# Attention input turned by VectorE and DRAM, score row spread by DMAs through DRAM, in a four-layer graph network

## Chip, cores and metric

One core of one Trainium2 chip. The metric is device microseconds of the whole kernel, taken as the median of several runs. Four chips served the experiments; each kernel was compared with the kernel before on the same chip (its medians there: 1815.4 to 1816.4 us).

Engine names: TensorE (PE in the profile, PEld for its weight loads), VectorE (DVE), ScalarE (ACT), GpSimd (POOL), SyncE (SP, the engine that issues nearly all DMAs here).

## The reference, cut

32 batches of 512 tokens with 128 features, everything in fp32, one adjacency matrix of 512 x 512. Each layer is `x = x + layer(relu(layernorm(x)))`.

- layer 0: normalised adjacency times input times a 128 x 128 matrix (GCN)
- layer 1: five steps of a gated recurrence; each step multiplies by the adjacency and applies three gates (GGNN)
- layers 2 and 3: attention over neighbours (GAT)

```python
h = jnp.einsum('bnf,fo->bno', x, W)
e_src, e_dst = h @ a_src, h @ a_dst                       # one score per token each
e = leaky_relu(e_src[:, :, None] + e_dst[:, None, :], 0.2)
e = where(adjacent, e, -inf)
out = softmax(e, -1) @ h
```

## The kernel before

A small scheduler in the kernel, run at build time, gives each operation an assumed cost and delay and lays down a fixed order for every engine. An engine works through its order, so one whose next instruction waits is idle, whatever stands behind it.

```python
plan = Plan({
    "bank": tiles(5, TOKENS, "bank", psum),               # single PSUM banks
    "cand": tiles(1, TOKENS, "cand", psum),
    "wide": tiles(1, [P, C, 2 * P], "wide", psum),        # a double bank, for attention
    "sq": tiles(2, ...), "far": tiles(4, [Q, W, Q, W * C], "far", dram),
    ...
```

The recurrent state (feature-major) gets back to token-major like this in every step: VectorE turns 32 x 32 blocks into `sq`, four DMAs write them to DRAM (`far`), a fifth reads them back in the right place (`h`).

```python
nc.vector.transpose(sq..., new...)
for k in range(Q):
    nc.sync.dma_start(far.t[:, :, k, :].rearrange("q i f -> i q f"), sq.t[k * W:(k + 1) * W])
nc.sync.dma_start(h.t, far.t.rearrange("q i k f -> (q i) k f"))
```

The attention layer turns its input on TensorE and spreads one score per token over all partitions on TensorE too:

```python
pT = to_features(y, ...)                  # 4 transposes on PE, L389, into a bank
gT = nc.vector.tensor_copy(pT)
q = gT @ w_aug                            # "heads": h and three score columns, L495
arg = q[:, :, D:D+3] * rstd;  h[:, :, D:D+3] = exp(arg);  k = h[:, :, D] * rstd
h[:, :, :D] = q[:, :, :D] * k
for c in range(C):                        # 4 transposes on PE, L508, into a bank
    nc.tensor.transpose(row.t[:, c, :], h.t[:, c, D + 2:D + 3].to_broadcast([P, P]), ident.t)
for j in range(C):                        # L511
    e[:, j, :] = max(row, h[:, j, D + 1]) * maskT[:, j, :]
p = e.T @ h                               # "mix", 16 matmuls, L518
```

The softmax here doesn't subtract the row's maximum and nothing guards it: scores larger than these inputs give would overflow.

## Time and profile before

| | before |
|---|---|
| median time, us | 1816.43 |
| span of the profiled run, us | 1814.0 |
| TensorE busy / idle, us | 1773.6 / 40.4 |
| of that idle: first 100 us / middle / after 1700 us | 11.3 / 1.4 / 27.7 |
| VectorE / ScalarE busy | 66% / 37% |
| mean granted TensorE clock | 0.996 |

Idle is the span less the busy time. The lines behind it stand in the prediction and are read there.

### The profile page before, as it was taken

To read this page: it belongs to the slowest core of one execution; us is meant where nothing else is said; L and a number is where in the kernel's file an instruction comes from. 1 tells how busy PE (TensorE), PEld (TensorE's weight loads), DVE (VectorE), ACT (ScalarE), POOL (GpSimd) and SP (SyncE) were. 2 spreads that over 40 slices of the span, in tenths; PEclk is the share of its full clock that TensorE was granted. 3 is DMA by queue.
4 is the path that set the end of the run, shared out by engine and by line. 5 is a ranking of instruction groups with operands and counts; after the bars stand their busy time and mean duration, and the time that the engine had idled before them with its cause. 6 is when DMAs were issued, how large, how long until landed. Compare 5 with 4: busy or idle time off the path is not lost.

```text
span 1814.0 us, 20223 instructions
## 1 busy us (share of the span) xinstructions
PE 1773.6 (98%) x6624; PEld 1143.2 (63%) x6624; DVE 1189.3 (66%) x2981; ACT 672.5 (37%) x1322; POOL 180.4 (10%) x168
## 2 busy tenths in 40 slices
PE   7999999999999999999999999999999999999985
PEld 4555565666665666765766657677666666666665
DVE  8554575577755767854867557677576667665665
ACT  4433344343433344333434334423444233333321
POOL 5100010011100110100111001010001000000000
PEclk9999999999999999999999999999999999999999
DMA  7121212212122212122121222112111221222210
GB/s 227 41 70 53 70 46 59 53 53 53 36 58 67 68 47 53 36 55 61 47 53 41 66 68 54 47 47 60 52 47 53 59 53 47 53 60 57 58 48 18
DMA packets 152266, 103.85 MB, mean 57 GB/s; under 512 B 15328, under 2 KB 131168, under 8 KB 152160
## 3 DMA queue, kind: packets, MB, share of 16 engines
q1 hardware_dynamic: 151872, 102.04, 21.3%
q8 instruction: 52, 0.85, 0.2%
q14 instruction: 54, 0.44, 0.1%
q10 hardware_dynamic: 288, 0.52, 0.1%
HBM read 52.17 MB, written 50.33 MB: 57 GB/s over the span
## 4 chain that ended last, share of the span: by engine, by line
PE 94%; DVE 3%; DMA 1%; issue 0%; POOL 0%; ACT 0%; SPq 0%; DVEq 0%; POOLq 0%; ACTq 0%
PE bank L397 36%; PE wide L518 13%; PE bank L441 8%; PE cand L448 8%; PE cand L449 8%; PE bank L434 8%; PE bank L435 7%; PE wide L495 3%; PE bank L389 2%; PE bank L508 1%; PE bank L413 1%; DVE e L511 1%; DVE st L356 1%; DMA h<-far 0%; DVE off L370 0%
## 5 line engine op out<-in xcount | busy, mean ns | idle before, releaser
L397 PE MATMUL bank<-adjT,h 128*128 128x512 f32 x1280 | 611.5, 605 | 0.6 <-DMA h<-far 0.6
L397 PEld LDWEIGHTS bank<-adjT,h 128*128 128x128 f32 x1280 | 385.7, 311 | 144.7 <-issue 36.0
L453 DVE TENSOR_TENSOR hv<-hv,hT 128x512 f32<-128x512 f32 x160 | 111.1, 694 | 295.3 <-ACT hv L451 294.9
L518 PEld LDWEIGHTS wide<-h_gat,e 128*128 128x128 f32 x2048 | 247.2, 195 | 47.0 <-issue 27.5
L363 POOL TENSOR_TENSOR rstd<-ve,mhalf 128x4 f32<-128x4 f32 x128 | 137.0, 1072 | 1318.4 <-DVE ve L361 367.1
L518 PE MATMUL wide<-h_gat,e 128*128 128x129 f32 x2048 | 250.1, 279 | 11.2 <-DVE h_gat L502 4.1
L399 ACT COPY m<-bank 128x512 f32<-128x512 f32 x192 | 112.1, 584 | 280.9 <-PE bank L397 280.0
L437 ACT ACTIVATE r<-bank,gate_bw 128x512 f32<-128x512 f32 x160 | 109.7, 686 | 260.2 <-PE bank L435 254.8
L439 DVE SCALAR_TENSOR_TENSOR rh<-r,hT 128x512 f32<-128x512 f32 x160 | 109.9, 687 | 137.5 <-ACT r L437 136.6
L511 DVE SCALAR_TENSOR_TENSOR e<-bank,h_gat,maskT 128x512 f32<-128x512 f32 x256 | 175.2, 738 | 13.7 <-PE bank L508 13.4
L443 ACT ACTIVATE z<-bank,gate_bw 128x512 f32<-128x512 f32 x160 | 109.8, 686 | 194.7 <-PE bank L441 194.7
L451 ACT ACTIVATE hv<-cand,gate_bw 128x512 f32<-128x512 f32 x160 | 109.9, 687 | 180.6 <-PE cand L449 180.3
L463 DVE STREAM_TRANSPOSE sq<-hT 128x512 f32<-128x512 f32 x160 | 164.7, 1029 | 4.4 <-DMA far<-sq 1.8
L441 PE MATMUL bank<-m,wT 128*128 128x512 f32 x320 | 163.9, 594 | 1.7 <-ACT r L437 1.7
L434 PE MATMUL bank<-m,wT 128*128 128x512 f32 x320 | 163.8, 593 | 1.4 <-ACT m L399 1.4
L448 PE MATMUL cand<-m,wT 128*128 128x512 f32 x320 | 163.5, 592 | 0.0
L449 PE MATMUL cand<-rh,wT 128*128 128x512 f32 x320 | 163.5, 592 | 0.0
L435 PE MATMUL bank<-hT,wT 128*128 128x512 f32 x320 | 163.4, 592 | 0.0
L397 PE MATMUL bank<-anT,y 128*128 128x512 f32 x256 | 122.8, 607 | 1.6 <-DVE x L415 0.9
L356 DVE BATCH_NORM_STATS2 st<-x 128x6 f32<-128x128 f32 x512 | 117.7, 279 | 1.6 <-DMA x<-in_x_dram 0.8
L456 DVE SCALAR_TENSOR_TENSOR hT<-hv,hT 128x512 f32<-128x512 f32 x160 | 110.3, 689 | 4.0 <-PE bank L441 0.5
L454 DVE SCALAR_TENSOR_TENSOR hv<-z,hv 128x512 f32<-128x512 f32 x160 | 110.2, 689 | 3.9 <-issue 0.2
(85 smaller groups left out, 1418.7 us busy)
## 6 DMA issues: line engine op xcount, KB each, us to landing
far<-sq SPq DMA_DIRECT2D x640, 64.0 KB, 1.8
h<-far SPq DMA_DIRECT2D x160, 256.0 KB, 2.6
x<-in_x_dram SPq DMA_DIRECT2D x32, 256.0 KB, 4.5
out_dram<-x SPq DMA_DIRECT2D x32, 256.0 KB, 2.2
e<-in_adj_dram ACTq DMA_DIRECT2D x2, 256.0 KB, 4.2
e<-in_adj_dram SPq DMA_DIRECT2D x2, 256.0 KB, 3.9
w<-in_L_gnn_w_w_dram SPq DMA_DIRECT2D x3, 128.0 KB, 3.8
u<-in_L_gnn_u_w_dram SPq DMA_DIRECT2D x2, 64.0 KB, 3.0
```

The lines of the kernel that those rows point to most:

```text
L356: op("DVE", 0.21, due, lambda c=c: nc.vector.bn_stats(st.t[:, c, :], xb.t[:, c, :]), r=[xb[c]], w=[st[c]])
L363: op("POOL", 1.0, due, lambda: nc.gpsimd.tensor_tensor(rstd.t, ve.t, mhalf.t, ALU.pow), r=[ve, mhalf], w=[rstd])
L397: op("PE", MM, due, lambda c=c: nc.tensor.matmul(flat(p.t), chunk(h, c), mT.t[:, c, :], start=(c == 0), stop=(c == C - 1)), r=[h[c] if len ...
L399: op("ACT", A, due, lambda: nc.scalar.copy(flat(m.t), flat(p.t)), r=[p], w=[m])
L434: nc.tensor.matmul(flat(gate.t), gates.t[:, 0, :], flat(m.t), start=True, stop=False)
L435: nc.tensor.matmul(flat(gate.t), gates.t[:, 1, :], flat(hT.t), start=False, stop=True)
L441: op("PE", MM, due + 0.3, lambda: nc.tensor.matmul(flat(gate.t), gates.t[:, 2, :], flat(m.t), start=False, stop=True, skip_group_check=Tru ...
L448: nc.tensor.matmul(flat(cand.t), gates.t[:, 3, :], flat(m.t), start=True, stop=False)
L449: nc.tensor.matmul(flat(cand.t), u5T.t[:, 0, :], flat(rh.t), start=False, stop=True)
L463: op("DVE", 0.61 if last else 1.0, due - 5, lambda: nc.vector.transpose(sq.t.rearrange(form, c=C), flat(new.t).rearrange("p (c q i) -> p q ...
L511: op("DVE", 0.68, due + 2, lambda j=j: nc.vector.scalar_tensor_tensor(e.t[:, j, :], flat(row.t), h.t[:, j, D + 1:D + 2], maskT[l].t[:, j, ...
L518: nc.tensor.matmul(p.t[:, c, :D + 1], e.t[:, j, c * P:(c + 1) * P], h.t[:, j, :D + 1], start=(j == 0), stop=(j == C - 1))
```

## The change

The intent is to take 448 transposes off TensorE, which is the bound. In 28 of 32 batches the input of attention takes the way that the recurrent state already takes (VectorE blocks, DRAM, back), and the score row is written to DRAM and read back by all partitions. The last four batches (`near`), whose latency ends the run, keep TensorE. The blocks leave tokens in a permuted order, so masks are permuted once through DRAM; the layer-norm scale moves into the ReLU, which removes two small VectorE operations. With the banks no longer needed for the transposes, two single banks become a second double bank. Only 16 buffers for x remain, to make room in SBUF.

```diff
-        "bank": tiles(5, TOKENS, "bank", psum),
+        "bank": tiles(3, TOKENS, "bank", psum),
-        "wide": tiles(1, [P, C, 2 * P], "wide", psum),
+        "wide": tiles(2, [P, C, 2 * P], "wide", psum),
+        "x": tiles(16, TOKENS, "x"),
+        "row": tiles(2, [P, N], "row"),
+        "line": tiles(4, [C, Q, W], "line", dram),
 ...
+    def shuttle(src, squares, dst, form, due, soon):     # the five DMAs above, as a function
 ...
     def gat(b, l, due):
-        pT = to_features(y, due + 1, gT)
+        near = b >= B - NEAR                              # NEAR = 4
+        if near: pT = to_features(y, due + 1, gT) ...
+        else:    shuttle(y, "p (c q j) -> p q c j", gT, "p q (c j) -> p q c j", due + 0.5, due)
 ...
+        else:
+            line = Val("line", C)
+            for c in range(C):
+                op("SP", 0.4, due + 1.5, lambda c=c: nc.sync.dma_start(
+                    line.t[c].rearrange("q i -> i q"), h.t[c * W:(c + 1) * W, :, D + 2]),
+                   r=[h[1]], w=[line[c]], delay=5)
+            op("SP", 0.4, due + 1.5, lambda: nc.sync.dma_start(
+                row.t, line.t.rearrange("c q i -> (c q i)").unsqueeze(0).to_broadcast([P, N])),
+               r=[line], w=[row, e], delay=4.5)
```

The line, one score column of `h`, four bytes in each of 32 partitions and four slots, goes to DRAM as 128 pieces of 4 bytes. Four such DMAs make one row.

More of the change, by code (lines that the diff above doesn't have):

```diff
@@ L20 @@
 Q = P // W
+NEAR = 4
 LANES = 4
@@ L181, in gnn_stack @@
         "hv": tiles(2, TOKENS, "hv"),
-        "gT": tiles(2, TOKENS, "gT"),
+        "gT": tiles(2, [P, Q, W * C], "gT"),
         "h_gat": tiles(3, [P, C, D + 3], "h_gat"),
+        "row": tiles(2, [P, N], "row"),
+        "line": tiles(4, [C, Q, W], "line", dram),
         "e": tiles(2, [P, C, N], "e"),
         "v": tiles(2, TOKENS, "v"),
+        "mask": tiles(2, [P, N], "mask", dtype=BF16),
         "st": tiles(4, [P, C, 6], "st"),
@@ L190, in gnn_stack @@
         "off": tiles(4, SMALL, "off"),
-        "arg": tiles(3, [P, C, 3], "arg"),
-        "k": tiles(3, SMALL, "k"),
         "rden": tiles(3, SMALL, "rden"),
@@ L230, in gnn_stack @@
     for b in range(B):
-        v = Val(None, C)
-        v.t = tiles(1, TOKENS, f"x{b}")[0]
-        op("SP", 0.95, -995 + b, lambda v=v, b=b: nc.sync.dma_start(v.t, x[b].rearrange("(c p) d -> p c d", p=P)),
+        v = Val("x", C)
+        op("SP", 0.95, max(-995 + b, STEPS * b - 20) if b >= 8 else -995 + b, lambda v=v, b=b: nc.sync.dma_start(v.t, x[b].rearrange("(c p) d -> p c d", p=P)),
            w=[v], delay=3)
@@ L292, in gnn_stack, with edges @@
     op("DVE", 4 * 0.7 + 4 * 0.25, -797, scale_rows, r=[adjT, dinv, drow, ident, dinv2], w=[anT])
-    maskT = {l: fixed([P, C, N], f"maskT{l}", dtype=BF16) for l in (2, 3)}
+    maskT = {l: fixed([P, Q, N], f"maskT{l}", C, dtype=BF16) for l in (2, 3)}
     for l in (2, 3):
-        op("DVE", 1.25, 5 + l, lambda l=l: nc.vector.tensor_scalar(maskT[l].t, adjT.t, 0.0, None, op0=ALU.is_gt),
-           r=[adjT], w=[maskT[l]])
-    def own_edges():
-        for m in range(C):
-            nc.vector.scalar_tensor_tensor(block(maskT[2].t, m), block(adjT.t, m), -1.0, ident.t,
-                                           op0=ALU.mult, op1=ALU.is_lt)
-    op("DVE", 4 * 0.25, 8, own_edges, r=[adjT, ident], w=[maskT[2]])
+        far = Val(None, C)
+        far.t = tiles(1, [Q, W, C, N], f"far_mask{l}", dram, BF16)[0]
+        for c in range(C):
+            part = Val("mask", 1)
+            def edges(l=l, c=c, part=part):
+                nc.vector.tensor_scalar(part.t, adjT.t[:, c, :], 0.0, None, op0=ALU.is_gt)
+                if l == 2:
+                    nc.vector.scalar_tensor_tensor(part.t[:, c * P:(c + 1) * P], block(adjT.t, c), -1.0, ident.t,
+                                                   op0=ALU.mult, op1=ALU.is_lt)
+            op("DVE", 0.35 if l == 3 else 0.6, 4 + l, edges, r=[adjT, ident], w=[part])
+            op("SP", 0.4, 4 + l, lambda c=c, far=far, part=part: nc.sync.dma_start(
+                far.t[:, :, c, :].rearrange("q i n -> (q i) n"), part.t), r=[part], w=[far[c]], delay=2.2)
+        for c in range(C):
+            op("SP", 0.4, 4 + l, lambda l=l, c=c, far=far: nc.sync.dma_start(
+                maskT[l].t[c * W:(c + 1) * W], far.t[:, :, c, :].rearrange("q i n -> i q n")),
+               r=[far], w=[maskT[l][c]], delay=2.2)
     ws = {k: fixed([P, D], k + "s") for k in ("w4", "w3", "w5")}
@@ L391, in to_features @@
         return p
+    def shuttle(src, squares, dst, form, due, soon):
+        sq, far = Val("sq"), Val("far", Q)
+        op("DVE", 0.61 if form == "p q (c j) -> p q c j" else 1.0, soon, lambda: nc.vector.transpose(
+            sq.t.rearrange(form, c=C), flat(src.t).rearrange(squares, c=C, q=Q)), r=[src], w=[sq])
+        for k in range(Q):
+            op("SP", 0.44, due, lambda k=k: nc.sync.dma_start(
+                far.t[:, :, k, :].rearrange("q i f -> i q f"), sq.t[k * W:(k + 1) * W]), r=[sq], w=[far[k]], delay=1.7)
+        op("SP", 0.4, due, lambda: nc.sync.dma_start(dst.t, far.t.rearrange("q i k f -> (q i) k f")),
+           r=[far], w=[dst], delay=2.5)
     def product(h, mT, due):
@@ L460, in step @@
         last = s == STEPS - 1
-        sq, far, h = Val("sq"), Val("far", Q), Val("h")
+        h = Val("h")
         form = "p q (c j) -> p q c j" if last else "p q (j c) -> p q c j"
-        op("DVE", 0.61 if last else 1.0, due - 5, lambda: nc.vector.transpose(
-            sq.t.rearrange(form, c=C), flat(new.t).rearrange("p (c q i) -> p q c i", c=C, q=Q)), r=[new], w=[sq])
-        for k in range(Q):
-            op("SP", 0.44, due, lambda k=k: nc.sync.dma_start(
-                far.t[:, :, k, :].rearrange("q i f -> i q f"), sq.t[k * W:(k + 1) * W]), r=[sq], w=[far[k]], delay=1.7)
-        op("SP", 0.4, due, lambda: nc.sync.dma_start(h.t, far.t.rearrange("q i k f -> (q i) k f")),
-           r=[far], w=[h], delay=2.5)
+        shuttle(new, "p (c q i) -> p q c i", h, form, due, due - 5)
         if last:
@@ L481, in gat @@
     def gat(b, l, due):
-        xb, y, off = xs[b], Val("y", C), Val("off")
-        mv, rstd = norm_stats(b, due)
-        op("DVE", 0.1, due, lambda: nc.vector.tensor_scalar_mul(off.t, mv.t[:, :, 0], -1.0), r=[mv], w=[off])
-        for c in range(C):
-            op("ACT", 0.32, due, lambda c=c: nc.scalar.activation(y.t[:, c, :], xb.t[:, c, :], AF.Relu, bias=off.t[:, c:c + 1]),
-               r=[xb[c], off], w=[y[c]])
-        gT, h = Val("gT"), Val("h_gat", 2)
-        pT = to_features(y, due + 1, gT)
-        op("DVE", V, due + 1, lambda: nc.vector.tensor_copy(flat(gT.t), flat(pT.t)), r=[pT], w=[gT])
-        q, arg, k = Val("wide"), Val("arg"), Val("k")
+        xb, y, gT, h, q = xs[b], Val("y", C), Val("gT"), Val("h_gat", 2), Val("wide")
+        norm_relu(b, y, due)
+        near = b >= B - NEAR
+        if near:
+            pT = to_features(y, due + 1, gT)
+            op("DVE", V, due + 1, lambda: nc.vector.tensor_copy(
+                gT.t.rearrange("p q (c i) -> p q c i", c=C), pT.t.rearrange("p c (q i) -> p q c i", q=Q)), r=[pT], w=[gT])
+        else:
+            shuttle(y, "p (c q j) -> p q c j", gT, "p q (c j) -> p q c j", due + 0.5, due)
         def heads():
@@ L495, in heads @@
                 nc.tensor.matmul(q.t[:, c, :D + 3], gT.t[:, c, :], w_aug[l].t, start=True, stop=True)
-        op("PE", C * MM1, due + 1, heads, r=[gT, w_aug[l]], w=[q, h])
-        op("DVE", 0.1, due + 1, lambda: nc.vector.tensor_mul(arg.t, q.t[:, :, D:D + 3], rstd.t[:, :, None].to_broadcast([P, C, 3])),
-           r=[q, rstd], w=[arg])
-        op("ACT", 0.22, due + 1, lambda: nc.scalar.activation(h.t[:, :, D:D + 3], arg.t, AF.Exp), r=[arg], w=[h[1]])
-        op("DVE", 0.1, due + 1, lambda: nc.vector.tensor_mul(k.t, h.t[:, :, D], rstd.t), r=[h[1], rstd], w=[k])
@@ L502, in gat @@
-        op("DVE", V, due + 1, lambda: nc.vector.tensor_mul(h.t[:, :, :D], q.t[:, :, :D], k.t[:, :, None].to_broadcast([P, C, D])),
-           r=[q, k], w=[h[0]])
-        row, e = Val("bank"), Val("e", C)
-        def spread():
+        op("PE", C * MM1, due + 1.5, heads, r=[gT, w_aug[l]], w=[q, h])
+        op("ACT", 0.22, due + 1, lambda: nc.scalar.activation(h.t[:, :, D:D + 3], q.t[:, :, D:D + 3], AF.Exp), r=[q], w=[h[1]])
+        op("DVE", V, due + 1.5, lambda: nc.vector.tensor_mul(
+            h.t[:, :, :D], q.t[:, :, :D], h.t[:, :, D:D + 1].to_broadcast([P, C, D])), r=[q, h[1]], w=[h[0]])
@@ new lines, in gat, with spread @@
+        row, e = Val("row"), Val("e", C)
+        if near:
+            pr = Val("bank")
+            def spread():
+                for k in range(Q):
+                    nc.tensor.transpose(pr.t[:, k, :], h.t[:, k, D + 2:D + 3].to_broadcast([P, P]), ident.t)
+            op("PE", C * TURN, due + 2, spread, r=[h[1], ident], w=[pr, row])
+            op("ACT", A, due + 2, lambda: nc.scalar.copy(
+                row.t.rearrange("p (c q i) -> p c q i", c=C, q=Q), pr.t.rearrange("p q (c i) -> p c q i", c=C)),
+               r=[pr], w=[row, e])
+        else:
+            line = Val("line", C)
@@ L507, in spread @@
             for c in range(C):
-                nc.tensor.transpose(row.t[:, c, :], h.t[:, c, D + 2:D + 3].to_broadcast([P, P]), ident.t)
-        op("PE", C * TURN, due + 2, spread, r=[h[1], ident], w=[row, e])
+                op("SP", 0.4, due + 1.5, lambda c=c: nc.sync.dma_start(
+                    line.t[c].rearrange("q i -> i q"), h.t[c * W:(c + 1) * W, :, D + 2]), r=[h[1]], w=[line[c]], delay=5)
+            op("SP", 0.4, due + 1.5, lambda: nc.sync.dma_start(
+                row.t, line.t.rearrange("c q i -> (c q i)").unsqueeze(0).to_broadcast([P, N])), r=[line], w=[row, e], delay=4.5)
@@ L510, in gat @@
         for j in range(C):
-            op("DVE", 0.68, due + 2, lambda j=j: nc.vector.scalar_tensor_tensor(
-                e.t[:, j, :], flat(row.t), h.t[:, j, D + 1:D + 2], maskT[l].t[:, j, :], op0=ALU.max, op1=ALU.mult),
+            op("DVE", 0.68, due + 3, lambda j=j: nc.vector.scalar_tensor_tensor(
+                e.t[:, j, :], row.t, h.t[:, j, D + 1:D + 2], maskT[l].t[:, j, :], op0=ALU.max, op1=ALU.mult),
                r=[row, h[1], maskT[l]], w=[e[j]])
@@ L519, in mix @@
                                      start=(j == 0), stop=(j == C - 1))
-            op("PE", C * MM1, due + 3, mix, r=[e, h], w=[p] if c == 0 else [p[c]])
-        op("DVE", 0.12, due + 3, lambda: nc.vector.reciprocal(rden.t, p.t[:, :, D]), r=[p], w=[rden])
+            op("PE", C * MM1, due + 4, mix, r=[e, h], w=[p] if c == 0 else [p[c]])
+        op("DVE", 0.12, due + 4, lambda: nc.vector.reciprocal(rden.t, p.t[:, :, D]), r=[p], w=[rden])
         if l == 2:
             v, n = Val("v"), Val("r")
-            op("DVE", V, due + 3, lambda: nc.vector.tensor_mul(v.t, p.t[:, :, :D], rden.t[:, :, None].to_broadcast([P, C, D])),
+            op("DVE", V, due + 4, lambda: nc.vector.tensor_mul(v.t, p.t[:, :, :D], rden.t[:, :, None].to_broadcast([P, C, D])),
                r=[p, rden], w=[v])
-            op("ACT", A, due + 3, lambda: nc.scalar.activation(flat(n.t), flat(v.t), AF.Exp), r=[v], w=[n])
-            op("DVE", V, due + 3, lambda: nc.vector.scalar_tensor_tensor(flat(v.t), flat(v.t), 0.0, flat(xb.t), op0=ALU.max, op1=ALU.add),
+            op("ACT", A, due + 4, lambda: nc.scalar.activation(flat(n.t), flat(v.t), AF.Exp), r=[v], w=[n])
+            op("DVE", V, due + 4, lambda: nc.vector.scalar_tensor_tensor(flat(v.t), flat(v.t), 0.0, flat(xb.t), op0=ALU.max, op1=ALU.add),
                r=[xb], w=[v])
-            op("DVE", V, due + 3, lambda: nc.vector.scalar_tensor_tensor(flat(xb.t), flat(n.t), 1.0, flat(v.t), op0=ALU.min, op1=ALU.add),
+            op("DVE", V, due + 4, lambda: nc.vector.scalar_tensor_tensor(flat(xb.t), flat(n.t), 1.0, flat(v.t), op0=ALU.min, op1=ALU.add),
                r=[n, v], w=[xb])
@@ L536, in finish @@
                                                    op0=ALU.mult, op1=ALU.add)
-            op("DVE", 4 * 0.28, due + 3, finish, r=[p, rden], w=[xb])
-            op("SP", 0.95, due + 3, lambda: nc.sync.dma_start(out[b].rearrange("(c p) d -> p c d", p=P), xb.t), r=[xb])
+            op("DVE", 4 * 0.28, due + 4, finish, r=[p, rden], w=[xb])
+            op("SP", 0.95, due + 4, lambda: nc.sync.dma_start(out[b].rearrange("(c p) d -> p c d", p=P), xb.t), r=[xb])
     for b in range(B):
@@ L544, in gnn_stack @@
         gat(b, 2, STEPS * b + LANES * (STEPS - 1) + 3)
-        gat(b, 3, STEPS * b + LANES * (STEPS - 1) + 7)
+        gat(b, 3, STEPS * b + LANES * (STEPS - 1) + 8)
     with tc.manual_schedule():
```

## The prediction

> **What bounds the kernel now.** I read, in this order: the busy totals and slices of the page, the table of stretches, the waits of TensorE, its timeline in the middle of the run, the groups by line, and the landing times of the DMAs.
>
> ```profile
> PE 1773.6 (98%) x6624; PEld 1143.2 (63%) x6624; DVE 1189.3 (66%) x2981; ACT 672.5 (37%) x1322; POOL 180.4 (10%) x168
> ...
> 0.00:100.00 100.00, 88.66 (x252) 1.00 0.44 127
> 100.00:1700.00 1600.00, 1598.64 (x5929) 1.00 0.21 54
> 1700.00:1814.00 114.00, 86.25 (x448) 0.93 0.14 38
> ...
> PE bank L434 <- ACT m L399: 0.7, 1, 0.7
> PE bank L397 <- DMA h<-far: 0.6, 2, 0.3
> ```
>
> The reader is to see that TensorE is busy for 1598.64 of the 1600 us from 100 to 1700 us, and that its only waits there are the two last lines, 1.3 us in all. Its idle time is 11.3 us in the first 100 us and 27.7 us in the last 114. So the middle is bound by what TensorE issues and by nothing else, and a TensorE instruction removed there is worth its issue interval, whatever the other engines do, as long as they keep up.
>
> The interval is not the duration in the table. The timeline of TensorE (start, busy, engine, line) shows it:
>
> ```profile
> 1101.01 2.00 PE L397 MATMUL bank<-adjT,h 128*128 128x512 f32 x4
> 1102.84 0.60 PE L508 MATMUL bank<-ident,h_gat 128*128 128x128 f32 x4
> 1103.28 0.60 PE L389 MATMUL bank<-ident,y 128*128 128x128 f32 x4
> 1103.72 1.14 PE L397 MATMUL bank<-adjT,h 128*128 128x512 f32 x2
> 1104.70 1.06 PE L495 MATMUL wide<-w_aug,gT 128*128 128x131 f32 x8
> ```
>
> Four transposes have a mean duration of about 0.27 us each, but the next group starts 0.44 us after the first of the four (1102.84, 1103.28, 1103.72): 0.11 us each. The median over all such groups of four between 60 and 1730 us is 0.44 us for L508 (the score row) and for L389 on y. The last lines show a second cost: two matmuls of L397 on h take 0.98 us to the next group there, and 0.86 us when their predecessor is a 512-column matmul (median of 42 groups). The groups tell why: this line's weights are read with a stride.
>
> ```profile
> L397 PEld LDWEIGHTS bank<-adjT,h 128*128 128x128 f32 x1280 | 385.7, 311 | 144.7 <-issue 36.0
> L453 DVE TENSOR_TENSOR hv<-hv,hT 128x512 f32<-128x512 f32 x160 | 111.1, 694 | 295.3 <-ACT hv L451 294.9
> L518 PEld LDWEIGHTS wide<-h_gat,e 128*128 128x128 f32 x2048 | 247.2, 195 | 47.0 <-issue 27.5
> ```
>
> A load of 311 ns does not fit under a 128-column predecessor, a load of 195 ns shows no such penalty. L453 is here for its idle time: VectorE waits 295 us in front of this one line, so it has room.
>
> **What the skill says.** The Trainium skill, "TensorE: Matmul & The Clock Gate", Part 4: PE-mode transpose, gives about 275 ns for a transpose in a kernel's context. The trace has 273 ns as the median duration, but the interval of 0.11 us decides here. The same page, LDWEIGHTS (loading the stationary operand), makes the load depend on the number of columns alone; the trace differs, 311 against 195 ns for the same 128 columns, and the measurement decides. "VectorE: DVE Perf Modes", The three transpose paths, says that VectorE turns only 32x32 blocks and writes SBUF; that is why the change needs DMAs to put the blocks in place. The trace has 693 ns (contiguous output) and 1099 ns (strided) for a 128x512 turn. "DMA: Bandwidth & Descriptors", Anatomy of one DMA, puts a fixed part of about 2 us before any size effect. The trace agrees: 2.1 us for 0.5 KB, 1.8 us for 64 KB, 2.6 us for 256 KB.
>
> ```profile
> far<-sq SPq DMA_DIRECT2D x640, 64.0 KB, 1.8
> h<-far SPq DMA_DIRECT2D x160, 256.0 KB, 2.6
> ...
> a_pair<-in_L_gnn_a_src_dram SPq DMA_DIRECT2D x2, 0.5 KB, 2.2
> ```
>
> **The change part by part.** There are 64 attention layers, two for each of 32 batches. The last four batches keep the old way, so 56 change.
>
> Removed from TensorE: 56 x (4 + 4) transposes. The built programs confirm it (transposes of y and h_gat go from 256 each to 32 each; nothing is added). 56 x 0.88 us = 49.3 us, all in the stretch that is 99.9% busy.
>
> Removed indirectly: the order of the built programs shows how often L397 on h starts behind a short instruction, 125 times before and 64 times after. 61 x 0.12 us = 7.3 us.
>
> VectorE: each of the 56 loses a gT copy (0.684 us) and gains a square turn (0.69), which is nothing. All 64 lose arg and k (0.162 + 0.171), 21 us. The 256 score operations (L511) read the row from SBUF in place of PSUM; L439, the same kind from SBUF, takes 0.687 us against 0.738, so some 11 us less in the 224 that change. The sum is about -30 us, off the path.
>
> ScalarE: the ReLU takes a scale as well, 391 to some 483 ns for 256 pieces, +24 us on an engine that is 37% busy. Off the path.
>
> DMA: 56 x (4 far + 1 gT + 4 line + 1 row) = 560 more issues of 0.43 us: SyncE's queue goes from 884 to 1460 issues in the built program, some 640 us of issuing in 1760. Traffic grows by 56 x 0.75 MB = 42 MB over 104; at the present cost, a DMA share of 21% becomes about 30%. Hidden, if nothing waits for it.
>
> Does something wait? From the attention's matmul on w_aug ("heads") to its first mix matmul, the new chain is: heads 0.9, exponential 0.2, gaps 0.3, four line issues 1.7, landing 2.1, row 2.6, four score operations 2.8 = 10.6 us (an estimate from the durations above). Counting TensorE work between those two points in the built order, with the intervals measured here, gives 15 to 30 us, median 18, for the 56 changed layers. That is 4 us of margin at the worst. Before, the same count gives 6 to 22 us for a chain of about 5 us, and TensorE did not wait at all in the middle. The order was laid for slower DMAs than these.
>
> PSUM: five single banks become three, but none is used any more for y, and the score row no longer occupies one for four score operations. A GGNN step holds a bank for its product (3.4 us plus the copy) and one for its gates (about 6 us), some 10 bank-us in 7.7 us of TensorE work, so three should do. The second double bank lets the heads of one layer start while another mixes.
>
> The end: before, 6.25 mixes are left behind the last GGNN matmul and 66 us pass, because one double bank passes from layer to layer and VectorE is 98% busy from 1770 to 1780. After, 7 mixes are left, in pairs over two double banks. I give it 3 us less idle time. For waits that I do not foresee in the middle I add 3 us.
>
> Sum: 1816.75 - 49.3 - 7.3 - 3 + 3 = 1760 us, 3.1% less.
>
> **The rivals.** (1) The row's way through DRAM is slower than I count: 512 pieces of 4 bytes per layer, and 128 partitions reading the same 2 KB. If line and row took 5 us each, the chain would be 16 us and the tightest layers would wait a few us each; SyncE and VectorE work in order, so the GGNN steps behind would be held too. 56 layers x 0.5 us gives 1788, "same". Against it: the 0.5 KB loads landed in 2.2 us, and the DMA engines are 21% busy. For it: no DMA of the trace before has this shape. (2) The three banks become the bound: the product of one lane waits for the evacuation of another. The sign would be waits of L421 or L458 for ScalarE. With 0.2 us in each of 160 steps it would be 1792. Against it: before, ScalarE waits for TensorE and not the other way round. (3) Only the removed transposes count and the 7.3 us do not appear, or the pairs in the tail crowd VectorE: 1767 to 1772. (4) The reverse: two double banks shorten the tail by 10 us or more, 1750.
>
> **Range and chances.** The saving of 49.3 us is certain in its count, so the time is 1767 without any second effect. Favourable ones (7 and up to 10 us) pull to 1750, waits push to 1776 before a rival is really at work. The 2% line is at 1780.4, which needs 20 us of new idle time in the middle or at the end; I give that one chance in ten. Slower by 2% would need 92 us of new waits: 0.01.
>
> **What would show it.** Right: TensorE idle under 6 us from 100 to 1700 us, transposes of y and h_gat 32 each, busy time down by some 50 us. Step two: the groups of L421 on h that follow a 512-column matmul are more, and busy time falls by more than 49. Wrong: waits of the mix (L546) for the score operations, themselves waiting for the row DMA; landing times of line and row above 4 us; waits of L421 or L458 for a bank; h landing later than 3.2 us; or more than 30 us idle in the tail.

## The result and the profile after

The changed kernel is correct and slower: 1961.55 us (1955.39 to 1962.28, four runs) against 1816.43, ratio 1.079 with a 95% interval of 1.077 to 1.081. Ratios are the mean time of one kernel's fast runs over that of the other's of the same rounds, so not quite the ratio of the medians. The prediction was 1760 us, with a range of 1750 to 1776.

From the page of the changed kernel and its table of stretches (length, TensorE busy with its count, granted clock, DMA share, GB/s):

```profile
PE 1788.2 (91%) x6176; PEld 1125.6 (57%) x6176; DVE 1180.4 (60%) x2859; ACT 692.7 (35%) x1330; POOL 185.3 (9%) x168
...
100.00:1850.00 1750.00, 1608.53 (x5453) 0.96 0.34 77
1850.00:1960.00 110.00, 91.85 (x473) 0.90 0.16 43
```

The 448 transposes are gone (6624 to 6176 matmuls), yet busy time rose, the middle that was full now has 141 us of idle time, and the granted clock is 0.96 there. The waits of TensorE (waited for, total us, times, longest):

```profile
PE wide L513 <- DMA gT<-far: 45.6, 15, 8.5
PE wide L546 <- DVE e L539: 36.0, 35, 6.0
PE cand L473 <- DVE rh L463: 30.8, 8, 10.8
PE bank L421 <- DMA h<-far: 15.9, 7, 4.6
```

L513 is the heads, L546 the mix, L473 a gate of the recurrence, L421 its product. The waits are spread over four places, of which only L546 belongs to the score row. What they share is seen in the landing times of the DMAs:

```profile
far<-sq SPq DMA_DIRECT2D x864, 64.0 KB, 1.8
h<-far SPq DMA_DIRECT2D x160, 256.0 KB, 2.6
gT<-far SPq DMA_DIRECT2D x56, 256.0 KB, 2.9
row<-line SPq DMA_DIRECT2D x56, 256.0 KB, 3.9
...
line<-h_gat SPq DMA_DIRECT2D x224, 0.5 KB, 7.2
```

The smallest transfer of all is the slowest, 7.2 us for 0.5 KB. And medians hide company. The three lines below are the last line of the view of one source line, for `far` in the kernel before, for `far` after, and for the line DMAs after (minimum, median, maximum):

```profile
DMA to landing us min/median/max: 1.6/1.8/4.2
DMA to landing us min/median/max: 1.6/1.8/11.8
DMA to landing us min/median/max: 5.7/7.2/12.4
```

The worst `far` went from 4.2 to 11.8 us. I sorted the trace's `far`, `h` and `gT` issues after 235 us, grouped as the timeline groups them, by how long after a line DMA they were issued. The numbers are the median over the groups of each group's median landing time:

| issued after the latest line DMA | far, us | h, us | gT, us |
|---|---|---|---|
| within 3 us | 6.3 (28 groups) | 8.1 (7) | 8.4 (8) |
| more than 10 us | 1.8 (140) | 2.6 (71) | 2.8 (25) |

So a DMA that has nothing to do with the score row lands about 5 us late if it stands right behind a line. One place in the timeline shows how this reaches TensorE, and what it costs twice:

```profile
581.25 1.02 PE L472 MATMUL cand<-m,wT 128*128 128x512 f32 x2
593.04 2.08 PE L473 MATMUL cand<-rh,wT 128*128 128x512 f32 x2 [10.77 <-DVE rh L463]
594.91 2.77 PE L421 MATMUL bank<-adjT,h 128*128 128x512 f32 x3
```

The chain of waits in that stretch runs: line DMAs, then `far` DMAs issued behind them that take 6.62 us, then the VectorE turn (L409) that needs the buffer they empty, then `rh`, which stands behind it in VectorE's order, then L473. After the 10.77 us of waiting, two matmuls take 2.08 us in place of 1.02. The Trainium skill, "TensorE: Matmul & The Clock Gate", Part 1: The HAM clock gate, says that the clock falls to half after an idle window of some 3.4 us; the trace agrees, with 2.08 against 1.02 us here and a mean clock of 0.958 over the run. All six matmuls with 512 columns that follow a gap of over 3.4 us in this trace take 1.21 to 1.22 us, twice the 0.61 us that those of L421 take on average. (The length of the window itself was not tested.)

### The profile page after: what moved, and what is told of

Read it like the earlier page. It is cut to its first block, busy times and chain, and to the rows that moved or that the text cites. A ratio compares the mean times of both kernels' runs of the same rounds, so it can differ in the third digit from the quotient of the medians.

```text
span 1959.2 us, 20126 instructions
## 1 busy us (share of the span) xinstructions
PE 1788.2 (91%) x6176; PEld 1125.6 (57%) x6176; DVE 1180.4 (60%) x2859; ACT 692.7 (35%) x1330; POOL 185.3 (9%) x168
## 4 chain that ended last, share of the span: by engine, by line
PE 61%; DMA 22%; DVE 8%; SPq 3%; ACT 3%; issue 2%; POOL 0%; DVEq 0%; ACTq 0%; POOLq 0%
PE bank L421 23%; PE wide L546 9%; DMA line<-h_gat 6%; DMA row<-line 5%; PE cand L473 5%; DMA far<-sq 5%; PE bank L458 5%; PE bank L459 5%; PE bank L465 5%; PE cand L472 5%; DVE e L539 2%; DMA gT<-far 2%; DMA h<-far 2%; DVE sq L409 2%; SPq L534 1%
## 5 line engine op out<-in xcount | busy, mean ns | idle before, releaser
L421 PE MATMUL bank<-adjT,h 128*128 128x512 f32 x1280 | 619.1, 612 | 18.8 <-DMA h<-far 15.9
L421 PEld LDWEIGHTS bank<-adjT,h 128*128 128x128 f32 x1280 | 390.3, 311 | 197.4 <-issue 70.7
L546 PE MATMUL wide<-h_gat,e 128*128 128x129 f32 x2048 | 271.0, 291 | 45.9 <-DVE e L539 36.0
L546 PEld LDWEIGHTS wide<-h_gat,e 128*128 128x128 f32 x2048 | 260.1, 204 | 82.8 <-DVE e L539 46.6
L539 DVE SCALAR_TENSOR_TENSOR e<-row,h_gat,maskT 128x512 f32<-128x512 f32 x256 | 181.8, 755 | 83.3 <-DMA row<-line 82.4
L409 DVE STREAM_TRANSPOSE sq<-hT 128x512 f32<-128x512 f32 x160 | 163.6, 1023 | 69.9 <-DMA far<-sq 66.2
L473 PE MATMUL cand<-rh,wT 128*128 128x512 f32 x320 | 169.3, 611 | 30.8 <-DVE rh L463 30.8
L385 ACT ACTIVATE y<-x,off,rstd 128x128 f32<-128x128 f32 x384 | 161.0, 484 | 60.7 <-DVE sq L409 27.6
L458 PE MATMUL bank<-m,wT 128*128 128x512 f32 x320 | 168.3, 608 | 0.2 <-ACT m L423 0.2
L465 PE MATMUL bank<-m,wT 128*128 128x512 f32 x320 | 165.8, 600 | 0.8 <-ACT r L461 0.8
L513 PE MATMUL wide<-w_aug,gT 128*128 128x131 f32 x512 | 76.4, 298 | 55.3 <-DMA gT<-far 45.6
L473 PEld LDWEIGHTS cand<-rh,wT 128*128 128x128 f32 x320 | 61.5, 195 | 110.7 <-issue 62.9
```

What stands on the lines that cost most here:

```text
L385: op("ACT", 0.32, due, lambda c=c: nc.scalar.activation(chunk(y, c), xb.t[:, c, :], AF.Relu, bias=off.t[:, c:c + 1], scale=rstd.t[:, c:c + ...
L409: op("DVE", 0.61 if form == "p q (c j) -> p q c j" else 1.0, soon, lambda: nc.vector.transpose(sq.t.rearrange(form, c=C), flat(src.t).rear ...
L421: op("PE", MM, due, lambda c=c: nc.tensor.matmul(flat(p.t), chunk(h, c), mT.t[:, c, :], start=(c == 0), stop=(c == C - 1)), r=[h[c] if len ...
L458: nc.tensor.matmul(flat(gate.t), gates.t[:, 0, :], flat(m.t), start=True, stop=False)
L465: op("PE", MM, due + 0.3, lambda: nc.tensor.matmul(flat(gate.t), gates.t[:, 2, :], flat(m.t), start=False, stop=True, skip_group_check=Tru ...
L473: nc.tensor.matmul(flat(cand.t), u5T.t[:, 0, :], flat(rh.t), start=False, stop=True)
```

## The experiments

Thirteen kernels ran. All computed the right result; the probe kernels' total times mean nothing.

### 1. Which part of the change

**a1_row_by_pe**: row spread by TensorE in all batches, input still turned through DRAM.

```diff
-        near = b >= B - NEAR
-        if near:                       # input
+        if b >= B - 4:                 # input
 ...
-        if near:                       # row
+        if True:                       # row
```

> Changed kernel, but the score row is spread by TensorE in all 32 batches; the attention input still goes through VectorE squares and DRAM. T1 (the 4-byte line DMAs are slow and clog the SyncE queue): the loss goes, 24.6 us of the transposes stay saved, so 1785 to 1800 us. T2 (three single PSUM banks are too few): still above 1900. T3 (the way of the attention input through DRAM is what comes late; its waits are the largest, 45.6 us): above 1880.

**a2_turn_by_pe**: the other way round (input `True`, row `b >= B - 4`).

> The other half: the attention input is turned by TensorE in all batches, the score row still goes by line and row DMAs through DRAM. T1: still slow, 1890 to 1960 us, line landing near 7 us. T2: above 1900. T3: back to 1790 to 1800.

**a3_all_by_pe**: both `True`.

> Both by TensorE in all batches, so what is left of the change is three single banks and two double ones, heads in permuted token order, masks through DRAM, 16 x buffers. T1 and T3: 1808 to 1822 us, as before. T2: 1850 or more, with waits of TensorE for ScalarE's evacuations.

**a4_line_512B**: the changed kernel, with one more VectorE operation that puts the 128 scores of each line into one partition. The scheduler's assumed delays stay.

```diff
+            op("DVE", 0.25, due + 1.5, lambda: nc.vector.transpose(
+                cols.t, h.t[:, :, D + 3 - W:]), r=[h], w=[cols])       # 32x32 turns
             for c in range(C):
                 op("SP", 0.4, due + 1.5, lambda c=c: nc.sync.dma_start(
-                    line.t[c].rearrange("q i -> i q"), h.t[c * W:(c + 1) * W, :, D + 2]),
+                    line.t[c].unsqueeze(0), cols.t[(c + 1) * W - 1:(c + 1) * W]),
                    ...
```

> The changed kernel with one addition: a VectorE 32x32 turn (128x128, estimate 0.3 us) puts each score line into one partition, so each of the four line DMAs moves one piece of 512 bytes in place of 128 of 4 bytes; the planned delays stay. T1: line landing 1.8 to 2.5 us, no stalled SyncE issues, 1760 to 1775 us, faster than before by 2 to 3%. T2 or T3: stays above 1880.

| kernel | median, us | ratio to before (95%) | TensorE busy / idle, us |
|---|---|---|---|
| before | 1816.35 | | 1773.6 / 40.4 |
| a1_row_by_pe | 1798.87 | 0.991 (0.989 to 0.992) | 1750.1 / 47.1 |
| a2_turn_by_pe | 1939.23 | 1.067 (1.065 to 1.070) | 1797.1 / 134.4 |
| a3_all_by_pe | 1798.82 | 0.990 (0.989 to 0.992) | 1766.5 / 29.9 |
| a4_line_512B | 1754.35 | 0.966 (0.965 to 0.968) | 1718.7 / 35.3 |

Every kernel with the 4-byte lines is slow, every kernel without them is faster than before (a1 and a3 by 1% only, but clear of the noise). Two expectations missed: a3 came 9 us below its range of 1808 to 1822, and a4 came 6 us below its 1760 to 1775. a4 differs from the changed kernel by the form of the line alone and is 207 us faster. The three single banks (T2) and the input's way through DRAM (T3) are out as causes: both are in a4. Its busy times and the stretch from 100 to 1650 us:

```profile
PE 1718.7 (98%) x6176; PEld 1096.7 (63%) x6176; DVE 1192.8 (68%) x2915; ACT 697.5 (40%) x1330; POOL 183.2 (10%) x168
...
100.00:1650.00 1550.00, 1543.39 (x5458) 1.00 0.32 87
```

TensorE runs the same 6176 matmuls as in the changed kernel in 69.5 us less of busy time (1788.2 - 1718.7): that is the price of the low clock. Busy time times mean clock is nearly the same in both, 1788.2 x 0.958 = 1713 and 1718.7 x 0.996 = 1712. Idle time differs by 135.7 us (171.0 - 35.3). The two make up the 205 us between the spans.

a1 fell in its range, but it gains nothing on a3, though it has 224 transposes fewer: busy time falls by 16.4 us and idle time rises by 17.2. Its order is another one, and I did not find which of its waits is to blame.

### 2. Why a line hurts: late rows, held-up queue, or something below

Three theories. L: only the row comes later than the order expects. S: SyncE issues in order, and the built program hands eight completion semaphores in turn to its DMAs, so slow lines hold up the issue of the next DMAs. J: the lines slow the other DMAs while these are in flight.

**b1_plan_slow**: the scheduler is told that a line lands after 9 us.

```diff
-                   r=[h[1]], w=[line[c]], delay=5)
+                   r=[h[1]], w=[line[c]], delay=9)
```

> The changed kernel, laid out by its scheduler with 9 us in place of 5 for the landing of a line DMA; the program is the same but for order. L (only the late row hurts: the order expects it too early): 1790 us or less. S (a slow line DMA holds up the DMAs behind it in SyncE's order) and J (the small pieces slow the other DMAs themselves): 1850 to 1950.

**b2_dead_lines**: a1 plus the line DMAs, which nothing reads.

> a1_row_by_pe (1799 us) plus the 4-byte line DMAs of 28 batches, which nothing reads. L: 1795 to 1805, since no row waits. S and J: 1860 to 1940, with TensorE waiting for h and gT DMAs and for VectorE.

**b4_one_line_dma**: one DMA for the row's 512 pieces; ScalarE restores the order afterwards.

```diff
-            for c in range(C):
-                nc.sync.dma_start(line.t[c].rearrange("q i -> i q"), h.t[c * W:(c + 1) * W, :, D + 2])
+            nc.sync.dma_start(line.t.rearrange("q p -> p q"), h.t[:, :, D + 2])      # line is [Q, P]
```

> The changed kernel with one line DMA of 512 pieces of 4 bytes in place of four of 128 (and a ScalarE copy of the row that puts it in order). S: a long DMA holds one of the eight completion semaphores and not four, so much returns: 1770 to 1830. J: the same pieces, so 1900 or more. L: 1900 or more if it lands no sooner than 7 us.

**b3_lines_by_pool**: `nc.gpsimd.dma_start` in place of `nc.sync.dma_start` for the lines.

> The changed kernel with the 4-byte line DMAs issued by GpSimd, whose queue and completion semaphores are its own. If the lines only hold up what stands behind them in SyncE's own queue (ring): far and h DMAs land in 1.8 and 2.6 us again, and the time is 1760 to 1800 us. If they hold up the 16 DMA engines as such: far DMAs still land 3 us or more late beside a line, and the time stays above 1880.

| kernel | median, us | ratio to before (95%) | line landing, us |
|---|---|---|---|
| b1_plan_slow | 1948.76 | 1.073 (1.071 to 1.075) | 7.3 |
| b2_dead_lines | 1922.27 | 1.058 (1.057 to 1.060) | 7.0 |
| b4_one_line_dma | 1997.96 | 1.100 (1.096 to 1.103) | 9.9 |
| b3_lines_by_pool | 1912.63 | 1.053 (1.050 to 1.056) | 7.2 |

L falls as the main cause. Telling the order that lines are slow gives back 13 us, and lines that nobody waits for still cost 123 us on top of a1. That leaves 84 of the 207 us, of which late rows may have a part: in the changed kernel TensorE waits 36.0 us for scores (L546). The waits of TensorE in b2 are of the same kind as in the changed kernel, without any row to wait for (here L514 is the heads and L422 the product):

```profile
PE wide L514 <- DMA gT<-far: 41.1, 8, 10.3
PE bank L422 <- DMA h<-far: 27.5, 7, 5.6
```

S falls as the main cause: my expectation of 1770 to 1830 us for a single DMA was wrong by 168 us or more, and lines on GpSimd's queue, with semaphores that SyncE does not use, leave b3 158 us slower than a4. In b3 the `far` groups issued by SyncE within 3 us of a line still land after 7.4 us (median of 24 groups), against 1.8 us more than 10 us away from one. S may have a part in it all the same. b3 gives back 49 us, though its order is another one too, and the waits of SyncE in the changed kernel have this line for `far` issues that need nothing from a line,

```profile
SPq L412 <- DMA line<-h_gat: 53.3, 23, 4.5
```

but what it waits for is the landing itself. So most of the slowdown lies below the issuing queues, in what they share; how much S and L add to it was not parted further.

### 3. What makes the line slow

**m1_probes** and **m2_probes** put probe DMAs ahead of the changed kernel, five of a form, each waiting for the one before of its form (`scatters` and `rows`: four or more in flight). The first of a form does not wait for the last of the form before it, so it may run beside it.

```diff
+    probe("column", [P, 1], ..., lambda t, k: nc.sync.dma_start(t, msrc.t[:, 0, D + 2:D + 3]))
+    probe("apart",    [P, 16], ...,  dma_start(t[:, :1], msrc.t[:, 0, D + 2:D + 3]))     # 64 B apart
+    probe("farapart", [P, 128], ..., dma_start(t[:, :1], msrc.t[:, 0, D + 2:D + 3]))     # 512 B apart
+    ...
```

> The changed kernel with DMA probes in front of everything (the time means nothing): each form five times, one after the other. Forms: one line DMA as the kernel has it (128 pieces of 4 bytes, SBUF to DRAM), four of them in flight as in the kernel, 128 pieces of 4 bytes to a contiguous column, 128 pieces of 16 bytes, four rows of 512 bytes, the row spread to 128 partitions, and a load of 128 pieces of 4 bytes. If the number of pieces written makes the line slow: scatter and column and quads alike, 4 us or more alone, rows about 2 us. If it is only the company of other DMAs: all about 2 us alone, and slow only with four in flight. Spread 2.6 to 4 us; the load 2.1 us, as in the trace of before.

> Probes again, one DMA at a time, each form five times, read by the distance between issues. The first probes gave 8.0 us for 128 pieces of 4 bytes in a column of DRAM, 3.3 us for 128 pieces of 16 bytes, 2.2 us for the same 4-byte column loaded. Now: 4-byte pieces side by side, 64 bytes apart and 512 bytes apart, 32 pieces only, pieces of 8, 16, 32, 64 and 512 bytes, and 4-byte pieces into SBUF. If each small write is slow by itself: 8 us also when apart, 3 to 4 us for 32 pieces. If small writes hinder their neighbours in one block of DRAM: about 2.5 us when 512 bytes apart. In both cases about 2 us into SBUF and for 512 bytes.

From SyncE's timeline in m1 (start, first to last issue, form): the kernel's own line form alone, and four of them in flight at a time.

```profile
1.44 28.26 SPq L243 DMA_DIRECT2D scatter<-msrc  x5
29.74 29.93 SPq L244 DMA_DIRECT2D scatters<-msrc  x20
```

One alone takes (28.26 - 0.3)/4 = 7.0 us from issue to issue, on an idle chip, and four in flight take no longer (five rounds in 29.93 us). It is slow by itself, not by company. m1 also had 128 pieces of 16 bytes, which I took for 3.3 us each; the first of them ran beside the last 4-byte column and waited 8.3 us, the others took 1.4 to 1.8. So the number of pieces does not make the line slow. The row alone took 3.0 to 3.3 us, the 4-byte load 1.9 to 2.0 (first ones left out). From the DMA view of m2 (pieces written, KB, median us from issue to landing):

```profile
lines<-msrc SPq DMA_DIRECT2D x5, 64.0 KB, 1.5
...
column<-msrc SPq DMA_DIRECT2D x5, 0.5 KB, 8.8
apart<-msrc SPq DMA_DIRECT2D x5, 0.5 KB, 1.4
farapart<-msrc SPq DMA_DIRECT2D x5, 0.5 KB, 1.4
quarter<-msrc SPq DMA_DIRECT2D x5, 0.1 KB, 5.4
pairs<-msrc SPq DMA_DIRECT2D x5, 1.0 KB, 3.4
quads<-msrc SPq DMA_DIRECT2D x5, 2.0 KB, 2.0
beats<-msrc SPq DMA_DIRECT2D x5, 4.0 KB, 1.4
blocks<-msrc SPq DMA_DIRECT2D x5, 8.0 KB, 1.4
onchip<-msrc SPq DMA_DIRECT2D x5, 0.5 KB, 1.7
```

| 128 pieces unless noted, to DRAM | form | us |
|---|---|---|
| 4 B, side by side | column | 8.8 |
| 4 B, 64 B apart | apart | 1.4 |
| 4 B, 512 B apart | farapart | 1.4 |
| 4 B, side by side, only 32 pieces | quarter | 5.4 |
| 8 B, side by side | pairs | 3.4 |
| 16 B, side by side | quads | 2.0 |
| 32 B and 64 B, side by side | beats, blocks | 1.4 |
| 512 B, side by side | lines | 1.5 |
| 4 B into SBUF | onchip | 1.7 |

Medians are needed here, because the first DMA of a form runs beside the last of the form before. The first `apart` was issued 0.36 us after the last `column` on the same queue, and landed only after it, as its minimum, median and maximum show:

```profile
DMA to landing us min/median/max: 1.4/1.4/8.9
```

That is the delay of section 2 on an otherwise idle chip: a DMA that takes 1.4 us lands after 8.9 behind a column of single words.

The same number of 4-byte pieces takes 8.8 or 1.4 us, and what decides is how near to each other they fall in DRAM. The first branch of what I expected (each small write is slow by itself) is out; the second holds (1.4 us at 512 B, where I had expected 2.5), and already 64 B apart, or with pieces of 32 B, the cost is gone. The Trainium skill, "DMA: Bandwidth & Descriptors", Specifications, says that below 512 B the DMA engine does a read-modify-write. No run here shows that step itself; 4-byte writes 64 or 512 B apart and 32-byte writes side by side land as soon as 512-byte ones, so a write below 512 B is not slow as such, only close beside others. That they wait for one another's turn at a block of DRAM would fit the numbers; it is argued, not shown.

**b5_dead_lines_apart**: b2 with the unread pieces 512 B apart; number, size, queue and semaphores as they were.

```diff
-        "line": tiles(4, [C, Q, W], "line", dram),
+        "line": tiles(4, [C, W, Q, P], "line", dram),
-                        line.t[c].rearrange("q i -> i q"), h.t[...]
+                        line.t[c, :, :, 0], h.t[...]
```

> b2_dead_lines (1922 us) with one change: the 4-byte pieces, which nothing reads, go 512 bytes apart in DRAM and no longer side by side; their number, size, queue and semaphores stay. The probes took 8.4 us side by side and 1.4 us apart. If the small writes into one block of DRAM are what holds up the other DMAs: 1795 to 1815 us as without lines (a1_row_by_pe, 1799), far landings near 1.8 us behind a line. If it is the number of pieces or of DMAs: 1880 or more.

1801.11 us (ratio 0.992, 0.990 to 0.993), against 1922.27 for b2 and 1798.87 for a1 without any lines. The DMA view of b5:

```profile
far<-sq SPq DMA_DIRECT2D x864, 64.0 KB, 1.8
...
line<-h_gat SPq DMA_DIRECT2D x224, 0.5 KB, 1.8
```

The line lands in 1.8 us, and `far` groups within 3 us behind a line have a median of 1.8 us (38 groups, maximum 3.0). The cost was neither the number of pieces nor the number of DMAs; it was the 4-byte writes side by side in DRAM. (The expectation quotes 8.4 us for the column, which is the mean from issue to issue.)

### 4. The other parts, and the better kernel

**c1_banks_alone**: the kernel before with three single and two double banks, nothing else.

> The kernel before with three single banks and two double ones, and nothing else of the change. a3_all_by_pe came to 1799 us, 17 us less than before, without any transpose removed. If that is the second double bank at the end of the run: 1797 to 1805 us, idle time of TensorE after 1700 us down by 10 or more. If it is the other parts (x buffers, masks, fused heads): 1812 to 1820.

1816.00 us, ratio 1.000 (0.998 to 1.002); the expectation of 1797 to 1805 failed. Idle time after 1700 us did fall, from 27.7 to 18.0 us, but in the stretch from 100 to 1700 us it rose from 1.4 to 13.5, in many short waits (the longest sums: the mix for its scores 3.3, a gate for `r` 2.7). Whether missing banks made them was not traced. In a3, which has the same banks, that stretch stays full (1.1 us of idle time). Of the 17.6 us by which its span is shorter than before, 10.5 are idle time, nearly all of it in the tail, and 7.1 are busy time, although no transpose was removed. Why a3 has no such waits (its row leaves the bank by one ScalarE copy, the heads are shorter) was not tested.

**a5_one_row_dma**: a4 with one line DMA of four 512 B pieces and assumed delays of 2.0 and 3.2 us.

> a4_line_512B (1754 us) with one line DMA of four pieces of 512 bytes in place of four DMAs, and planned delays of 2.0 and 3.2 us, nearer to what was measured. 1748 to 1758 us; the middle is already within 7 us of full.

1759.21 us, ratio 0.969 (0.967 to 0.970): 5 us slower than a4, just outside the expected range. A plan nearer to the measured delays did not help. a4, 1754.35 us, is the best kernel and beats both.

## Why the prediction was wrong

**The step that failed** is the cost of the line DMA, in the paragraph "Does something wait?": "four line issues 1.7, landing 2.1". The 2.1 us came from loads of 128 pieces of 4 bytes, from DRAM to SBUF; the line is a store of such pieces. It landed after 7.2 us. The row took 3.9 us in place of 2.6. The chain of 10.6 us was really about 17 (10.6 + 5.1 + 1.3), more than the tightest 15 us of work laid over it. The other half of the same step is the overlap: the paragraph "DMA" gave the lines only issue time and bytes, and called the rest "Hidden, if nothing waits for it".

**The larger miss** is what rival 1 left out. It named the small pieces and 5 us each, but counted only the layers' own waits (56 x 0.5 us) and the engines behind in order. b2 shows that most of the loss (123 of 207 us) comes without any such wait: the other DMAs land 5 us late beside a line. Two of the prediction's signs of being wrong came, the mix's wait for scores and the late line; the median landing of `h` stayed at 2.6 us and hid the 8.1 us behind a line. The argument "the DMA engines are 21% busy" against the rival was worth nothing, because busy share does not show what a write makes others wait for; it rose to only 33% in the slow kernel.

**A term that was missing**: low clock after long waits, 69.5 us of busy time.

**What held.** a4 keeps the prediction's plan but for the form of the line (and one small VectorE operation per layer), and takes 1754 us against 1760. The landing times of its lines are missing in its trace. The 49.3 and 7.3 us: busy time fell by 54.9 (1773.6 - 1718.7); in a4's built order 68 groups of L397's kind start behind a short instruction, against 125, so the two terms make 49.3 + 57 x 0.12 = 56.1. a3 helps to part them: with every transpose left it has 89 such starts, and 7.1 us less busy time than before; a4 has 47.8 us less than a3, without the 448 transposes. So the 49.3 us were near, and at least part of the second term came with the other order and not with the transposes removed. The tail was mis-sized: idle time is 17 us in a4 after 1650 us against 28 before after 1700, a gain of 11 us and not 3. In the middle a4 is idle for 6.6 us, where the prediction had 1.4 + 3. That the sum came so near is in part luck: the larger gain in the tail covers the other two misses. Three banks sufficed (rival 2 did not come).

**Small misses.** The score operations did not get faster with the row in SBUF (755 ns after, 738 before; I had assumed 687), so VectorE's busy time fell by 9 us and not 30. ScalarE rose by 20 us (24 predicted). None of this was on the path.

## What to carry to other kernels

A DMA's cost has to be taken from a transfer of the same direction, piece size and spacing: the load of 4-byte pieces took 2.1 us, the store of such pieces 7.2. Never write a column of single words to neighbouring places in DRAM: turn it in SBUF first, so that the pieces are longer (here 512 bytes, by one VectorE operation per layer, worth 207 us against the changed kernel; in the probes 32 bytes were enough). 64 bytes between the words did as well in the probe, but how fast a row is read back from such words was not tested. When waits appear in many unrelated places, compare the maximum landing time of unrelated DMAs, not the median, and sort them by what was in flight beside them.

## What the Trainium skill lacked or had wrong

- "DMA: Bandwidth & Descriptors" (Specifications) has the 512 B threshold for line rate, but nothing on the spacing of small writes: 128 writes of 4 B landed after 8.8 us side by side and after 1.4 us at 64 B or 512 B; 128 writes of 32 B side by side also took 1.4 us.
- No page has what such writes cost unrelated DMAs: `far` landed after 6.3 us in place of 1.8 behind a line on the same queue, and after 7.4 us with the lines on GpSimd's queue.
- "DMA: Bandwidth & Descriptors" (Anatomy of one DMA) gives a fixed part of about 2 us for the GpSimd path; DMAs issued by SyncE landed after 1.4 to 1.7 us on an idle chip, for 0.5 to 64 KB.
- "TensorE: Matmul & The Clock Gate" (LDWEIGHTS) has the load depend on columns alone: it took 311 ns with strided weights and 195 ns without, for the same 128 columns, and two 512-column matmuls with strided weights took 0.12 us longer behind a 128-column one.
- The same page (Part 4) gives a transpose's duration, about 275 ns, which the trace confirms (273 ns), but not the interval in a stream, which is what removing one is worth: 0.11 us.
